# Causal attention of a decoder's first layer: the mask made in the score banks, maxima subtracted by halves

## The chip, the cores and the metric

The kernel runs on one core of one Trainium2 chip. A core has five instruction queues that run side by side: TensorE (PE, with its weight loads shown as PEld), VectorE (DVE), ScalarE (ACT), GpSimd (POOL) and SyncE (SP), the last used here for issuing transfers only. Each queue is worked in order; semaphores tie the queues together. Matrix products land in PSUM, eight banks of 128 x 512 fp32, and everything else lives in SBUF. The metric is the device time of the whole program in microseconds, median of several runs.

## The reference

The program is a decoder of four layers, each with self-attention, cross-attention and a feed-forward part, over x of 8 batches, 128 tokens and 256 features. The change is in the very first part:

```python
q = split_heads(lin(x, Wq, bq))          # x: layer-normed; 16 heads of 16
k = split_heads(lin(x, Wk, bk))
v = split_heads(lin(x, Wv, bv))
attn = jnp.einsum('bhqd,bhkd->bhqk', q, k) * scale          # scale = 1/4
attn = jnp.where(causal[None, None], attn, -jnp.inf)
attn = jax.nn.softmax(attn, axis=-1)
out = jnp.einsum('bhqk,bhkd->bhqd', attn, v)
out = out.transpose(0, 1, 3, 2).reshape(Bx, Tx, Cx)
return lin(out, Wp, bp)
```

Its result is added to x, and the next parts go on from there. Every later part needs the one before, so there is no work that could be done ahead of this one but loads, constants and products of weights.

## The kernel before, in words

**The start.** `decoder` (L2448) issues loads of constants, of x and of the context, and sets a few constants on GpSimd. GpSimd also sends a small table `less_own` to DRAM (L2501) and loads the byte mask of the context, `mu` (L2510), for later layers; VectorE turns it into fp32 (L2513) and derives two more tables (L2514, L2515). `mu` lives in a pool of its own that is closed again, and the weights' pool opens in its place. Then the twelve parts are called one after the other. Outside hand-ordered blocks the framework orders the instructions of each engine by itself; a block under `manual_schedule` keeps the order in which the code gives them.

**The first attention, `l0_attn` (L224).** The weights are loaded by SyncE (`weights`, L96): `w` with four matrices and `r` with biases, followed by the next part's `w` and `r` and two large pieces `st`. After the norm of x and its transposes (L191), eight groups of products (L46, tile `ps_mm`) give the queries `qT` and the keys `kb`; ScalarE and VectorE copy them out of PSUM (L247, L250, L253). `kb` holds every key twice, with the odd or the even head of a pair masked to zero, so that one product over 32 rows gives one head's scores. Then the values `va` are made (L258, L261), with a column of ones beside each head's 16 values: the product with the exponentials gives the sum of a row along with its values.

**The steps.** What follows goes over the 8 batches in a software pipeline: `in_step` (L379) gives, for each step t, each stage for batch t minus the stage's lag, all in one hand-ordered block. The stages, with their lags before the change, are:

- `score` (0): eight products (L209) fill a tile of four PSUM banks, 128 queries by 16 heads by 128 keys; VectorE adds the causal mask from the constants while it copies them to `s` (L280). There is one such tile, so the next batch's scores wait for this copy. In the call for batch 2, `clear_rows` (L1011) is called first: it writes zeros to the 8.4 MB DRAM buffer `rows_in` of a much later part, by a transfer that GpSimd issues (L1014).
- `less_max` (0): VectorE takes each row's maximum (L285), GpSimd subtracts it (L286).
- `exp` (1): ScalarE's exponential over all 16 heads (L301).
- `values` (2): `round_about` (L337) transposes the four groups of heads (L345), ScalarE copies them out (`pT`, L347), and products with `va` (L293) give the tile `ps_po`.
- `copied`, `turn`, `divided`, `project` and the add (3): `ps_po` is copied by ScalarE (L367) and transposed back (L375), VectorE divides by the sums (L312, L316), TensorE projects (L46, tile `ps_o`), VectorE adds to x (L195), and the next norm's statistics are taken (L155, L156) by batch.

With a largest lag of 3, eight batches take eleven steps. PSUM is full: four banks for scores, two for transposes, one for `ps_po`, one for the rest.

Of the kernel before, what the change touches and what calls it, by code (L numbers as in the profile page):

```python
# [8 lines left out]
F32 = mybir.dt.float32  # L9
BF16 = mybir.dt.bfloat16  # L10
# [3 lines left out]
AF = mybir.ActivationFunctionType  # L14
ALU = mybir.AluOpType
AX = mybir.AxisListType

P = 128
# [14 lines left out]
C_ID, C_LE, C_GT, C_CAUS, C_BO16, C_ONES = 0, 128, 256, 384, 512, 640  # L33
# [9 lines left out]
def mm(nc, out, pairs):  # L43

    for i, (lhsT, rhs) in enumerate(pairs):
        nc.tensor.matmul(out, lhsT, rhs, start=(i == 0), stop=(i == len(pairs) - 1))  # L46
# [151 lines left out]
def tok(b):  # L198
    return slice(b * S, (b + 1) * S)


def scores(k, psc, q, kb):


    for r in range(4):
        rows = slice(32 * r, 32 * r + 32)
        rhs = kb[rows]
        n = rhs.shape[1] * rhs.shape[2]
        k.nc.tensor.matmul(psc(r, n), q[rows], rhs, start=True, stop=True)  # L209
# [14 lines left out]
def l0_attn(k):  # L224
    nc, a = k.nc, k.a
    w, r_ = k.weights(a["p0"], a["r0"])
    wq, wk, wv, wp = (w[:, i * 512 : (i + 1) * 512].rearrange("p (c n) -> p c n", c=NC) for i in range(4))
    bq, bk = w[:, 2048:2050], w[:, 2050:2052]
    bv, bp = r_[:, 0:256], r_[:, 256:512]
    _, xnT = k.norm(bp)  # L230
    H, HD = 16, 16
    with k.tc.tile_pool(name="l0a", bufs=2) as wk_:
        qT = wk_.tile([P, NC, T], F32, name="qT", bufs=1)
        kb = wk_.tile([P, NC, 2, T], F32, name="kb", bufs=1)
        va = wk_.tile([P, B, 4, 4, 32], F32, name="va", bufs=1)
        nc.gpsimd.memset(va, 0.0)
        nc.gpsimd.memset(va[:, :, :, :, HD : HD + 1], 1.0)
        bkm = k.sm.tile([P, NC, 2], F32, name="bkm")
        nc.vector.tensor_tensor(
            bkm, bk.unsqueeze(2).to_broadcast([P, NC, 2]), k.m16.unsqueeze(1).to_broadcast([P, NC, 2]), ALU.mult  # L240
        )
        for g in range(2):
            ts_ = slice(g * 512, (g + 1) * 512)
            for o in range(NC):
                pm = k.mmt()
                mm(nc, pm, [(wq[:, c, o * P : (o + 1) * P], xnT[:, c, ts_]) for c in range(NC)])
                nc.scalar.activation(qT[:, o, ts_], pm, AF.Identity, bias=bq[:, o : o + 1])  # L247
                pm = k.mmt()
                mm(nc, pm, [(wk[:, c, o * P : (o + 1) * P], xnT[:, c, ts_]) for c in range(NC)])
                nc.scalar.activation(  # L250
                    kb[:, o, 0, ts_], pm, AF.Identity, bias=bkm[:, o, 0:1], scale=k.m16[:, 0:1]
                )
                nc.vector.tensor_scalar(  # L253
                    kb[:, o, 1, ts_], pm, k.m16[:, 1:2], bkm[:, o, 1:2], ALU.mult, ALU.add
                )
        for b in range(B):
            pv = k.ot()
            mm(nc, pv, [(xnT[:, c, tok(b)], wv[:, c, :]) for c in range(NC)])  # L258
            for o in range(NC):
                cs = slice(o * P, (o + 1) * P)  # L260
                nc.vector.tensor_tensor(  # L261
                    va[:, b, 2 * o : 2 * o + 2, :, 0:HD].rearrange("p j r d -> p r j d"),
                    pv[:, cs].rearrange("p (r j d) -> p r j d", r=4, d=HD),
                    bv[:, cs].rearrange("p (r j d) -> p r j d", r=4, d=HD),
                    ALU.add,
                )
        caus = k.c[:, C_CAUS : C_CAUS + P].unsqueeze(1).to_broadcast([P, H, P])
        k.banks({"tr": 2, "po": 1, "o": 1})
        S_, PO, OS, PB, OB, PY = {}, {}, {}, {}, {}, {}
        act = nc.scalar.copy  # L270

        def score(b):
            if b == 2:
                clear_rows(k)
            psc = k.sct()
            for o in range(NC):
                scores(k, lambda r, n: psc[:, r, o * 256 : o * 256 + n], qT[:, o, tok(b)], kb[:, o, :, tok(b)])
            s = S_[b] = wk_.tile([P, 4, 4, P], F32, name="s", bufs=4)
            sv = s.rearrange("p r g t -> p (r g) t")
            nc.vector.tensor_tensor(sv, psc.rearrange("p r (g t) -> p (r g) t", t=P), caus, ALU.add)  # L280

        def less_max(b):
            sv = S_[b].rearrange("p r g t -> p (r g) t")
            mx = k.sm.tile([P, H], F32, name="mx")
            nc.vector.tensor_reduce(mx, sv, AX.X, ALU.max)  # L285
            nc.gpsimd.tensor_tensor(sv, sv, mx.unsqueeze(2).to_broadcast([P, H, P]), ALU.subtract)  # L286

        def values(b):
            po = PO[b] = k.pot()

            def use(g, pT):
                for r in range(4):
                    nc.tensor.matmul(  # L293
                        po[32 * r : 32 * r + 32, g, :], va[:, b, g, r, :], pT[:, r, :], start=True, stop=True
                    )

            round_about(k, wk_, lambda g: S_[b][:, :, g, :], [act] * 4, use)

        def exp(b):
            sf = S_[b].rearrange("p r g t -> p (r g t)")  # L300
            nc.scalar.activation(sf, sf, AF.Exp, scale=HD**-0.5)  # L301

        def copied(b):
            OS[b] = back(k, wk_, PO[b])

        def turn(b):
            PB[b] = back_turned(k, OS[b])

        def divided(b):
            pb = PB[b].rearrange("p g (r e) -> p g r e", e=32)  # L310
            rec = k.sm.tile([P, 4, 4], F32, name="rec")
            nc.vector.reciprocal(rec, pb[:, :, :, HD])  # L312
            ob = OB[b] = wk_.tile([P, NC, 4, 2, HD], F32, name="ob")
            for o in range(NC):
                js = slice(2 * o, 2 * o + 2)
                nc.vector.tensor_tensor(  # L316
                    ob[:, o].rearrange("p r j d -> p j r d"),
                    pb[:, js, :, 0:HD],
                    rec[:, js, :].unsqueeze(3).to_broadcast([P, 2, 4, HD]),
                    ALU.mult,  # L320
                )

        def project(b):


            ov = OB[b].rearrange("p o r j d -> p (o r j d)").rearrange("p (t s) -> p s t", s=2)
            py = PY[b] = k.ot()
            mm(nc, py, [(ov[:, s_, :], wp[:, s_, :]) for s_ in range(2)])

        in_step(  # L330
            k, B,
            (3, copied), (3, turn), (0, score), (3, divided), (0, less_max),
            (2, values), (1, exp), (3, project), (3, lambda b: k.add_x(b, PY[b])),
        )


def round_about(k, wk_, src, copies, use):  # L337


    done = {}  # L340
    for g in range(6):
        if g < 4:
            pt = k.trt()
            for r in range(4):
                k.nc.tensor.transpose(pt[:, r, :], src(g)[:, r, :], k.ident)  # L345
            done[g] = wk_.tile([P, 4, P], F32, name="pT", bufs=3)
            copies[g](done[g], pt)  # L347
        if g >= 2:
            use(g - 2, done[g - 2])


def all_turned(k, wk_, src, copies):
# [11 lines left out]
def back(k, wk_, po):  # L364

    os_ = wk_.tile([P, 4, P], F32, name="os", bufs=4)
    k.nc.scalar.copy(os_, po)  # L367
    return os_


def back_turned(k, os_):

    pb = k.ot((P, 4, P))
    for g in range(4):
        k.nc.tensor.transpose(pb[:, g, :], os_[:, g, :], k.ident)  # L375
    return pb
# [432 lines left out]
class Heads:  # L809
# [13 lines left out]
    def turn_p(self, u):  # L823

        k = self.k
        pt = self.bank("tr", bufs=2)
        p = self.p.pop(u)
        for j in range(4):
            k.nc.tensor.transpose(pt[:, j, :], p[:, j, :], k.ident)
        self.pT[u] = self.sbuf("pT")  # L830
        k.nc.scalar.copy(self.pT[u], pt)  # L831
# [179 lines left out]
def clear_rows(k):  # L1011

    n = k.rows_in.shape[0] // P
    k.nc.gpsimd.dma_start(  # L1014
        k.rows_in.rearrange("(n p) d -> p n d", p=P), k.zero_rows.unsqueeze(1).to_broadcast([P, n, ROW])
    )
# [451 lines left out]
class L2Keys:  # L1468
# [139 lines left out]
    def values(self, b):  # L1608
        k = self.k
        pv = k.ot((P, 2, D))  # L1610
        for t, wv in enumerate((self.wvm, self.wvd)):
            mm(k.nc, pv[:, t, :], [(k.ctxT[:, b, :], wv)])
        for t in range(2):
            k.nc.scalar.activation(
                self.va[:, b, :, t, 0:16], pv[:, t, :].rearrange("p (h d) -> p h d", d=16), AF.Copy, scale=self.ends[t]
            )
# [1120 lines left out]
```

## Time and profile before

| what | us |
|---|---|
| median of 3 runs | 1948.71 (1945.85, 1948.71, 1960.44) |
| profiled execution, its own time | 1957.12 |
| its span | 1955.3 |
| PE busy in the span | 1717.8 (88%) |
| DVE busy | 1203.0 (62%) |
| ACT busy | 1037.7 (53%) |
| POOL busy | 365.8 (19%) |
| first products of `l0_attn` begin | 25.47 |
| first scores begin | 49.2 |
| last add to x ends | 130.7 |

All durations come from that one profiled execution. In the lines of a timeline the first number is the start from the span's beginning, the second the time that the line took, both in us; then engine, source line, operation, the tiles as out<-in with partitions x elements, and how many instructions the line merges. In square brackets stands how long the engine was idle before it and what ended that. In the lines of the chain of work only start, length and what are given. "SPq" and "POOLq" are the issuing of transfers, and "DMA" is time that passed until a transfer had landed.

### The profile page before, as it was taken

The numbers are of one execution on the slowest core, as the hardware profiler recorded it, in microseconds if no ns is written. First come the engines' busy times: TensorE is split into PE (matmuls) and PEld (weight loads), VectorE is DVE, ScalarE is ACT, GpSimd is POOL, SyncE is SP. The second block draws the span as 40 slices with busy tenths as digits, with TensorE's granted clock in tenths as the row PEclk, the third lists the DMA queues.
The fourth block names the chain that finished last, engine by engine and source line by source line (L and its number), as shares of the span: only waits on it lengthen the run. The fifth ranks groups of instructions, "written<-read, shape, count | busy, mean of one in ns | idle before, by whom it ended". The sixth has DMA issues, their size and how long they took to land.

```text
span 1955.3 us, 25181 instructions
## 1 busy us (share of the span) xinstructions
PE 1717.8 (88%) x9471; PEld 1136.2 (58%) x9477; DVE 1203.0 (62%) x2374; ACT 1037.7 (53%) x1711; POOL 365.8 (19%) x359
## 2 busy tenths in 40 slices
PE   5776977667999986998788989999999997999999
PEld 3453655444666653664466545555555556888667
DVE  4766778856677752326756767677676775454423
ACT  2445854434667741225464377778777763343432
POOL 3543542201121222332002000000000001333200
PEclk9896988878999997998999999999999998999989
DMA  4600026305000022111001110101101004000000
GB/s 135 177 25 1 2 97 209 111 1 215 1 12 6 12 82 105 50 41 51 17 1 36 17 50 18 33 18 34 34 18 34 18 1 162 1 1 1 1 1 22
DMA packets 38970, 90.29 MB, mean 46 GB/s; under 512 B 6865, under 2 KB 19490, under 8 KB 37186
## 3 DMA queue, kind: packets, MB, share of 16 engines
q1 hardware_dynamic: 31266, 69.43, 10.4%
q0 software_dynamic: 5488, 17.67, 3.0%
q8 instruction: 76, 1.25, 0.3%
q10 hardware_dynamic: 2096, 1.57, 0.3%
q14 instruction: 44, 0.36, 0.1%
HBM read 67.15 MB, written 21.51 MB: 45 GB/s over the span
## 4 chain that ended last, share of the span: by engine, by line
PE 68%; DVE 14%; ACT 11%; issue 3%; POOL 2%; DMA 1%; ACTq 0%; DVEq 0%; SPq 0%; POOLq 0%
PE ps_xz L46 9%; PE ps_o L46 7%; PE ps_o L2077 6%; PE ps_o L848 5%; PE ps_mm L46 5%; PE ps_q L46 5%; PE ps_h L46 4%; PE ps_u L46 3%; PE ps_sc L46 3%; PE ps_y L46 2%; PE ps_ty L46 2%; PE ps_xz L1994 2%; DVE mx L511 2%; PE ps_ty L2015 2%; PE ps_sc L209 2%
## 5 line engine op out<-in xcount | busy, mean ns | idle before, releaser
L46 PE MATMUL ps_xz<-xnT,wxz 128*128 128x512 f32 x512 | 237.1, 607 | 0.3 <-ACT ee L1997 0.3
L46 PEld LDWEIGHTS ps_xz<-xnT,wxz 128*128 128x128 f32 x512 | 93.3, 192 | 103.9 <-issue 101.9
L1974 DVE SCALAR_TENSOR_TENSOR xc<-pad,w,xc 128x1024 f32<-128x1024 f32 x96 | 123.1, 1282 | 30.5 <-ACT xc L1968 28.7
L2077 PE MATMUL ps_o<-wo,yg 128*128 128x256 f32 x512 | 128.0, 395 | 1.5 <-DVE yg L2056 1.5
L848 PE MATMUL ps_o<-wvo,uT 128*128 128x256 f32 x512 | 122.6, 383 | 0.0
L848 PEld LDWEIGHTS ps_o<-wvo,uT 128*128 128x128 f32 x512 | 98.5, 193 | 40.7 <-issue 30.3
L1997 ACT ACTIVATE ee<-ps_xz,sgn 128x512 f32<-128x512 f32 x128 | 87.1, 689 | 60.2 <-PE ps_xz L1994 60.2
L2077 PEld LDWEIGHTS ps_o<-wo,yg 128*128 128x128 f32 x512 | 93.5, 192 | 25.4 <-issue 12.9
L2017 DVE TENSOR_TENSOR dtx<-ps_ty,dt 128x512 f32<-128x512 f32 x64 | 41.4, 687 | 90.1 <-PE ps_ty L2015 89.9
L2369 POOL MEMSET gb<- 128x160 f32 x1 | 0.2, 231 | 504.1 <-PE ps_ty L46 504.1
L46 PE MATMUL ps_h<-moe,xT 128*128 x184 | 85.1, 606 | 0.9 <-DVE xT L1244 0.8
L2007 DVE TENSOR_TENSOR ee<-ee,gT 128x2048 f32<-128x2048 f32 x32 | 73.2, 2288 | 8.9 <-ACT ee L2003 8.9
L46 PE MATMUL ps_u<-pT,cx 128*128 128x512 f32 x128 | 70.0, 629 | 6.8 <-ACT pT L831 6.7
L947 ACT ACTIVATE s<-ps_sc,mx,rqs 128x128 f32<-128x128 f32 x128 | 48.1, 456 | 49.5 <-DVE rs_t L129 48.0
L2003 ACT ACTIVATE ee<-ee,sgn 128x1024 f32<-128x1024 f32 x64 | 73.0, 1145 | 0.2
L955 POOL TENSOR_TENSOR s<-s,sums 128x512 f32<-128x512 f32 x32 | 33.3, 1040 | 207.7 <-DVE sums L954 66.6
L512 POOL TENSOR_TENSOR s<-s,mx 128x2048 f32<-128x2048 f32 x16 | 57.8, 3610 | 53.6 <-DVE mx L511 53.6
L1258 DVE TENSOR_TENSOR h<-ps_h,sl 128x512 f32<-128x512 f32 x23 | 15.9, 692 | 82.2 <-PE ps_h L46 82.2
L46 PEld LDWEIGHTS ps_q<-xnT,wqk 128*128 128x128 f32 x512 | 64.3, 199 | 2.8 <-DVE xnT L62 1.0
L46 PE MATMUL ps_q<-xnT,wqk 128*128 128x128 f32 x512 | 64.8, 282 | 0.6 <-DVE xnT L62 0.6
L46 PE MATMUL ps_ty<-ee,dtx 128*64 128x128 f32 x1024 | 63.0, 276 | 2.3 <-DVE ee L2007 2.2
L358 PE MATMUL ps_tr<-consts,s 128*128 128x128 f32 x384 | 55.7, 290 | 8.4 <-ACT s L1726 3.3
(599 smaller groups left out, 4038.3 us busy)
## 6 DMA issues: line engine op xcount, KB each, us to landing
moe<-in_p SPq DMA_DIRECT2D x24, 512.0 KB
rows_in<-zero_rows POOLq DMA_DIRECT2D x1, 8385.0 KB, 34.4
wxz<-in_p9s SPq DMA_DIRECT2D x32, 256.0 KB
fold_vo<-in_p SPq DMA_DIRECT2D x8, 512.0 KB
wvo<-fold_out SPq DMA_DIRECT2D x16, 256.0 KB
wvo<-wvo SPq DMA_DIRECT2D x2, 2048.0 KB
wo<-in_p9s SPq DMA_DIRECT2D x16, 256.0 KB
st<-in_p SPq DMA_DIRECT2D x3, 1024.0 KB
```

What stands on the lines that cost most here:

```text
L46: nc.tensor.matmul(out, lhsT, rhs, start=(i == 0), stop=(i == len(pairs) - 1))
L209: k.nc.tensor.matmul(psc(r, n), q[rows], rhs, start=True, stop=True)
L358: k.nc.tensor.transpose(pt[:, r, :], src(g)[:, r, :], k.ident)
L512: nc.gpsimd.tensor_tensor(sv, sv, mx.unsqueeze(2).to_broadcast([P, 16, P]), ALU.subtract)
L848: k.nc.tensor.matmul(self.po[b], uT[:, j, :], self.wvo[:, 4 * hg + j, :], start=hg + j == 0, stop=hg + j == 6)
L947: nc.scalar.activation(s[:, j, :], psc[:, j, :], AF.Exp, scale=rs[:, j : j + 1], bias=mx[:, j : j + 1])
L1974: nc.vector.scalar_tensor_tensor(XC[n], (PAD[n] if n in PAD else pads[n % 2])[:, :, t : t + S], cw[:, n, t : t + 1], XC[n], ALU.mult, ALU.add)
L1997: nc.scalar.activation(e, pm, AF.Relu, scale=sgn[:, at : at + 1])
L2003: nc.scalar.activation(EE[n][:, h], EE[n][:, h], AF.Exp, scale=sgn[:, at : at + 1])
L2007: nc.vector.tensor_tensor(EE[n], EE[n], gT.unsqueeze(1).to_broadcast([P, 2, B, S]), ALU.mult)
L2017: nc.vector.tensor_tensor(DTX[n][:, bs], pt.rearrange("p (b h d) -> p b h d", b=4, d=HD), dt_[:, bs, 2 * n : 2 * n + 2].unsqueeze(3).to_br ...
L2077: nc.tensor.matmul(PO[b // 2][:, b % 2 * D : (b % 2 + 1) * D], YG[n][:, tok(b)], WO[n // 2][:, n % 2, :], start=False, stop=n == 31 and b ...
```

## The change

Only `l0_attn` is changed, and `round_about` goes, as nothing else used it. The causal mask becomes a bf16 tile; four products of the identity with that tile, repeated four times along the free axis, begin each bank of scores, and the scores are added on top of it in PSUM. VectorE takes the maxima of the heads of half of each bank straight from PSUM and subtracts them on the way to `s`, then does the other half later in the step; GpSimd no longer takes part. The exponential is given by halves too, in the same step as the scores, and everything behind it moves up by one: the largest lag is 2, so that there are ten steps. The order inside a step is a new one, with the transposes and value products of the batch before between the two halves.

```diff
-        caus = k.c[:, C_CAUS : C_CAUS + P].unsqueeze(1).to_broadcast([P, H, P])
+        caus = wk_.tile([P, P], BF16, name="caus", bufs=1)
+        nc.vector.tensor_copy(caus, k.c[:, C_CAUS : C_CAUS + P])
...
         def score(b):
             if b == 2:
                 clear_rows(k)
-            psc = k.sct()
+
+            psc = SC[b] = k.sct()
+            for r in range(4):
+                nc.tensor.matmul(
+                    psc[:, r, :], k.ident_b, caus.unsqueeze(1).to_broadcast([P, 4, P]), start=True, stop=False
+                )
             for o in range(NC):
-                scores(k, lambda r, n: psc[:, r, o * 256 : o * 256 + n], qT[:, o, tok(b)], kb[:, o, :, tok(b)])
-            s = S_[b] = wk_.tile([P, 4, 4, P], F32, name="s", bufs=4)
-            sv = s.rearrange("p r g t -> p (r g) t")
-            nc.vector.tensor_tensor(sv, psc.rearrange("p r (g t) -> p (r g) t", t=P), caus, ALU.add)
-
-        def less_max(b):
-            sv = S_[b].rearrange("p r g t -> p (r g) t")
-            mx = k.sm.tile([P, H], F32, name="mx")
-            nc.vector.tensor_reduce(mx, sv, AX.X, ALU.max)
-            nc.gpsimd.tensor_tensor(sv, sv, mx.unsqueeze(2).to_broadcast([P, H, P]), ALU.subtract)
...
                 for r in range(4):
+                    rows = slice(32 * r, 32 * r + 32)
                     nc.tensor.matmul(
...
+                        psc[:, r, o * 256 : o * 256 + 256],
+                        qT[rows, o, tok(b)],
+                        kb[rows, o, :, tok(b)],
+                        start=False,
+                        stop=(o == 1),
                     )
...
+        def less_max(o):
+            def f(b):
+                js = slice(2 * o, 2 * o + 2)
+                bank = SC[b].rearrange("p r (g t) -> p r g t", t=P)[:, :, js, :]
+                mx = MX[b][:, :, js]
+                nc.vector.tensor_reduce(mx, bank, AX.X, ALU.max)
+                nc.vector.tensor_tensor(
+                    S_[b][:, :, js, :], bank, mx.unsqueeze(3).to_broadcast([P, 4, 2, P]), ALU.subtract
+                )
+
+            return f
+
+        def exp(o):
+            def f(b):
+                sf = S_[b][:, :, 2 * o : 2 * o + 2, :]
+                nc.scalar.activation(sf, sf, AF.Exp, scale=HD**-0.5)
+
+            return f
...
         in_step(
             k, B,
-            (3, copied), (3, turn), (0, score), (3, divided), (0, less_max),
-            (2, values), (1, exp), (3, project), (3, lambda b: k.add_x(b, PY[b])),
+            (0, score), (2, turn), (1, turn_p((0, 1))), (0, less_max(0)), (2, divided), (0, exp(0)),
+            (1, turn_p((2,))), (1, values((0,))), (1, turn_p((3,))), (1, values((1,))), (2, project),
+            (0, less_max(1)), (1, values((2, 3))), (2, lambda b: k.add_x(b, PY[b])), (1, copied), (0, exp(1)),
         )
```

`turn_p` and the new `values` hold what `round_about` did, for the groups that they are given: transposes and a copy by ScalarE, and the products with `va`.

More of the change, by code (lines that the diff above doesn't have):

```diff
@@ L266, in l0_attn @@
                 )
-        caus = k.c[:, C_CAUS : C_CAUS + P].unsqueeze(1).to_broadcast([P, H, P])
+        caus = wk_.tile([P, P], BF16, name="caus", bufs=1)
+        nc.vector.tensor_copy(caus, k.c[:, C_CAUS : C_CAUS + P])
         k.banks({"tr": 2, "po": 1, "o": 1})
-        S_, PO, OS, PB, OB, PY = {}, {}, {}, {}, {}, {}
-        act = nc.scalar.copy
+        S_, MX, SC, PT, PO, OS, PB, OB, PY = {}, {}, {}, {}, {}, {}, {}, {}, {}
         def score(b):
@@ L288, in values @@
-        def values(b):
-            po = PO[b] = k.pot()
-            def use(g, pT):
+            psc = SC[b] = k.sct()
[3 more added lines that the diff above has]
+                )
+            for o in range(NC):
                 for r in range(4):
+                    rows = slice(32 * r, 32 * r + 32)
                     nc.tensor.matmul(
-                        po[32 * r : 32 * r + 32, g, :], va[:, b, g, r, :], pT[:, r, :], start=True, stop=True
-                    )
-            round_about(k, wk_, lambda g: S_[b][:, :, g, :], [act] * 4, use)
@@ L299, in exp @@
-        def exp(b):
-            sf = S_[b].rearrange("p r g t -> p (r g t)")
-            nc.scalar.activation(sf, sf, AF.Exp, scale=HD**-0.5)
+                        psc[:, r, o * 256 : o * 256 + 256],
[3 more added lines that the diff above has]
+                        stop=(o == 1),
+                    )
+            S_[b] = wk_.tile([P, 4, 4, P], F32, name="s", bufs=3)
+            MX[b] = k.sm.tile([P, 4, 4], F32, name="mx")
@@ new lines, in turn_p, with f, values @@
+        def turn_p(some):
+            def f(b):
+                for g in some:
+                    pt = k.trt()
+                    for r in range(4):
+                        nc.tensor.transpose(pt[:, r, :], S_[b][:, r, g, :], k.ident)
+                    PT[b, g] = wk_.tile([P, 4, P], F32, name="pT", bufs=4)
+                    nc.scalar.copy(PT[b, g], pt)
+            return f
+        def values(some):
+            def f(b):
+                if some[0] == 0:
+                    PO[b] = k.pot()
+                for g in some:
+                    pT = PT.pop((b, g))
+                    for r in range(4):
+                        nc.tensor.matmul(
+                            PO[b][32 * r : 32 * r + 32, g, :], va[:, b, g, r, :], pT[:, r, :], start=True, stop=True
+                        )
+            return f
@@ L331, in l0_attn @@
             k, B,
-            (3, copied), (3, turn), (0, score), (3, divided), (0, less_max),
-            (2, values), (1, exp), (3, project), (3, lambda b: k.add_x(b, PY[b])),
-        )
[L337 to L349, printed above, removed]
+            (0, score), (2, turn), (1, turn_p((0, 1))), (0, less_max(0)), (2, divided), (0, exp(0)),
+            (1, turn_p((2,))), (1, values((0,))), (1, turn_p((3,))), (1, values((1,))), (2, project),
+            (0, less_max(1)), (1, values((2, 3))), (2, lambda b: k.add_x(b, PY[b])), (1, copied), (0, exp(1)),
+        )
 def all_turned(k, wk_, src, copies):
```

## The prediction

> **What bounds the kernel now.** The change touches one stage, the first attention of a 1955.3 us span on one core, so I read in this order: the chain of work that ended last, for the first 130 us; the queues of GpSimd and SyncE for the same stretch; the DMA view around the one large GpSimd transfer; VectorE's timeline of one attention step. First the chain (start us, us, what):
>
> ```profile
> 18.95 0.54 issue
> 19.50 0.69 DVE mb L2513
> 20.21 5.22 DMA w<-in_p
> 25.43 0.04 issue
> 25.47 16.07 PE ps_mm L46 x32
> ```
>
> Everything from 20 us on hangs on the weight load `w`, and that load starts as VectorE's cast of the mask (L2513) ends: `w` sits in the memory that the mask tile `mu` leaves, so SyncE waits for the mask's landing and its cast. The queues (start us, us, queue, operation):
>
> ```profile
> 10.54 0.72 POOL L2501 DMA_DIRECT2D less_own<-less_own_rows  x1
> 13.20 0.62 POOL L2510 DMA_DIRECT2D mu<-in_mask_BxS_bf  x1 [1.94 <-DMA less_own<-less_own_rows]
> 27.23 5.50 POOL L184 TENSOR_TENSOR x<-x,r 128x256 f32<-128x256 f32 x8 [13.41 <-DMA r<-in_r]
> ...
> 59.60 3.61 POOL L286 TENSOR_TENSOR s<-s,mx 128x2048 f32<-128x2048 f32 x1 [0.91 <-DVE mx L285]
> 63.15 2.95 POOL L1014 DMA_DIRECT2D rows_in<-zero_rows  x1
> ...
> 20.21 0.33 SPq L101 DMA_DIRECT2D w<-in_p  x1
> ```
>
> The zero fill of `rows_in` (L1014) is issued at 63.15, long after the mask at 13.20, because it stands behind two subtractions of GpSimd. The DMA view, us from issue to landing in the last column:
>
> ```profile
> rows_in<-zero_rows POOLq DMA_DIRECT2D x1, 8385.0 KB, 34.4
> mu<-in_mask_BxS_bf POOLq DMA_DIRECT2D x1, 128.0 KB, 3.2
> q0 software_dynamic: 2176, 8.78, 23.5%
> ```
>
> All GpSimd transfers go through one queue, q0. Last, VectorE in a steady step of the attention:
>
> ```profile
> 87.34 2.29 DVE L280 TENSOR_TENSOR s<-ps_sc,consts 128x2048 f32<-128x2048 f32 x1 [1.48 <-PE ps_sc L209]
> 89.55 0.25 DVE L312 RECIPROCAL rec<-ps_o 128x16 f32<-128x16 f32 x1
> 89.83 0.49 DVE L316 TENSOR_TENSOR ob<-ps_o,rec 128x128 f32<-128x128 f32 x2
> 90.23 2.27 DVE L285 TENSOR_REDUCE mx<-s 128x16 f32<-128x2048 f32 x1
> 92.43 0.41 DVE L195 TENSOR_TENSOR x<-ps_o,x 128x256 f32<-128x256 f32 x1
> 95.00 2.29 DVE L280 TENSOR_TENSOR s<-ps_sc,consts 128x2048 f32<-128x2048 f32 x1 [1.48 <-PE ps_sc L209]
> ```
>
> A step is 95.00 - 87.34 = 7.66 us, with 6.18 us of VectorE work and 1.48 us in which it waits for scores. On the chain, the step runs through ScalarE (exponential, copies of `pT` and `os`) and TensorE. The first scores are made at 49.2, the last `x` is added at 130.7.
>
> **Part 1: the zero fill moves.** `clear_rows` is called inside score(2). Before, GpSimd's hand-ordered subtractions held it back. After, GpSimd has no other work in that block, and the built program has the zero fill directly after the transfer of `less_own` and ahead of the mask's. It waits for nothing: its source is set at 0.87 us. So it is issued at 10.54 + 0.72 = 11.3. In the trace its packets ran from 66.7 to 96.4, that is from 3.5 us after issue and for 29.7 us (8.59 MB, 289 GB/s); at 11.3 that gives 14.8 to 44.5, on engines that are otherwise nearly idle then (mean share 0.14 at 10 to 15 us, 0.07 at 15 to 20).
>
> What does the mask's transfer do behind it? It is now issued at 14.3, once the fill's 2.95 us on GpSimd are over. The row alone says 3.2 us, so 17.5, two us ahead of the cast at 19.5: no cost. But the row is of an empty queue. The Trainium skill, "DMA: Bandwidth & Descriptors", section "Queues, rings and completion order", says that each DMA engine takes the descriptors of one queue in order and shares its time only between queues; its section "SWDGE vs HWDGE vs iDMA" gives GpSimd a single queue, as the page's q0 does. By the rule the mask's 128 KB come after all 8.4 MB. I take the rule, as nothing in this trace shows two GpSimd transfers overtaking each other. The mask then moves at 44.5 and lands some 2 us later (3.2 us less what the issue takes): 46.5. Bounds: 45.3 (right with the last packet and a short tail) to 48.9 (zero fill landed at 11.3 + 34.4 = 45.7, and the full 3.2 after it).
>
> Behind that wait stand, on VectorE, L2513 to L2515, the small product `bkm`, and all copies of `kb`; on SyncE, every weight load of the first layers (`w`, `r`, `w`, `r`, two `st`). Nothing can be done meanwhile: norm and transposes end at 19. Cast 46.55 to 47.2, `w` issued at 47.25, landed after the same 5.22 us at 52.5. TensorE starts at 52.5 instead of 25.47: **+27.0 us** (25.8 to 29.4). What follows shifts as one piece, since the loads that it needs are issued behind `w`. Freeing the engines at 66 to 96 is worth nothing: nothing else moved then. TensorE's longer rest adds no slow start, as it idles 6.6 us ahead of 25.47 today too.
>
> **Part 2: the attention steps.** Removed per batch: L280 and L285 on VectorE (2.29 + 2.27), L286 on GpSimd (3.61), one exponential of 1.91. Added: two maxima and two subtractions of 128x1024 read from the score bank, two exponentials of half size on ScalarE, four 128x512 bf16 matmuls for the mask. L1713 and L1720 do just such a maximum and subtraction from a score bank: 0.415 us for 256 elements and 2.02 us for 1792, so 1.04 ns an element and 1.21 us for 1024, some 1.17 from start to start. Bounds: 1.12 by that line's slope with no more overhead, 1.28 by L1974's mean for 128x1024; over 32 instructions -1.5 to +3.5 us. For the mask the nearest row is the bf16 128x512 group, eight of which took 1.89 us at full clock: 4 x 0.24 = 0.95 us. Bounds: 0.87 (by the slope from five in 1.24 us to those eight) and 1.9 at half clock; over eight steps -0.6 to +7.6 us.
>
> A new loop now sets the step. The four score banks have one buffer, and VectorE reads them until its second subtraction, so the next mask and scores can start only then, and VectorE waits for them: 4 x 1.17 + reciprocal and two products 1.1 = 5.8, then mask 0.95, scores 1.1 (16 records in 1.15 us today), handovers 0.12. That is 7.95 us, against 7.66. The add of `x` with its statistics (1.06 us) lies beside TensorE's 2.1. TensorE has 7.4 us of work in a step (2.05, transposes 16 x 0.14 and 0.6, values 1.5, projection 1.1), ScalarE about 4.8: neither sets it. GpSimd's 28.9 us go, worth nothing by themselves.
>
> From a start at 49.2 as today: first maxima at 51.3, two steps without division at 6.95, five at 7.95, and the norm of the first four batches in between (6 us of VectorE, of which 4.8 show): the eighth batch begins at 109.7, plus 2 us for TensorE's half clock after its first waits (the granted clock is 0.53 at 53 to 63.5 today too, for the same reason): 111.7, against 107.2. From there to the last `x` today's drain takes 23.5 us; with ten steps for eleven I count 5.8 of VectorE, 1 exponential, transposes, copies, values, `os`, turn, division, projection and add, and the previous batch's tail between: 16 to 17.5, so 128.5 to 129. Against 130.7: **-2 us**, with the bounds above -4 to +9. The mask's cast to bf16 (128x128, under 0.3 us) lies in VectorE's idle time near 10 us; uncovered it costs that 0.3. `round_about` going costs nothing.
>
> **The sum.** +27.0 - 2.0 = +25 us. Against the profiled execution (1957.12 us, span 1955.3) this gives 1982; that execution is 8.4 us over the median of the three runs, 1948.71, but inside their 1945.85 to 1960.44. On the median: **1974 us**.
>
> **Rivals.** *The mask overtakes the fill* (not slower by what can be told). If GpSimd's transfers are served side by side, the mask lands near 17.5 and `w` is issued at 20.2 as today; but its queue then shares the engines with 7.0 MB of fill. The loads from 20.2 on are 4.2 MB in some 12.5 us; with half to two thirds of the engines they need 20 to 26, the second `st` lands at 41 to 46 and VectorE, whose sum L599 of `st` stands ahead of three copies of `kb`, holds the last projection's bank: +5 to +10. With -2 that is +6: 1955. It decides if the mask is in before 25 us or so. For it: each transfer has its own semaphore; against it: one queue in the page. *The steps stay at half clock:* TensorE's gaps of 4.9 us after each of the first scores keep it at 0.5 for several steps, the loop then has 4.1 instead of 2.05 and TensorE is itself the bound: +8 for four such steps, 1982. Against it: with 7.4 of 7.95 us busy it has fewer gaps than today, when it recovers at 73.7. *The attention gains what it can:* with VectorE alone as bound (6.9 a step) it ends 9 us earlier, and if the mask overtakes as well, the kernel comes to 1943.
>
> **How the numbers follow.** Forecast 0.80, half clock 0.08, overtaking 0.10, attention at its best with overtaking 0.02. About 1%, 19.5 us, is what a measurement of this kernel can tell from no change. Slower by over 1%: 0.80 x 0.95 + 0.08 = 0.84; within 1%: 0.14; faster: 0.02. The forecast's own range is 1970 to 1982 (+27.0 from 25.8 to 29.4, -2 from -4 to +4, the rest of the upper bound being the half clock's); with half clock at the top and some of the runs' scatter below, 1965 to 1984 leaves about 2 in 10 out.
>
> **What would show it.** The chain has the mask's transfer ahead of L2513, cast at 46 to 48, TensorE's first projection at 52 to 54, GpSimd's zero fill at 11.3. The step is 7.7 to 8.3 us with VectorE waiting about 1 us for scores once a step, and the stretch from first score to last add 77 to 86 us (81.5 today). A cast near 19.5 makes it wrong by 20 us; a stretch over 90 us says that the loop's TensorE part was underrated.

## The result and the profile after

| what | before | after |
|---|---|---|
| median | 1950.83 (4 runs, 1945.85 to 1960.44) | 1976.35 (4 runs, 1973.26 to 1976.99) |
| span of the profiled execution | 1955.3 | 1975.1 |
| first projection of `l0_attn` begins | 25.47 | 52.35 |
| first score product (after: first mask product) | 49.2 | 75.50 |
| last add to x ends | 130.7 | 151.25 |
| from the last add to the end of the span | 1824.6 | 1823.9 |

The changed kernel is slower: the ratio is 1.0122, with a 95% interval of 1.008 to 1.0163. The two spans differ by 19.8 us, and all of that is there when the last x is added: 151.25 - 130.7 = 20.5 us. Behind that point the two executions take the same time within 1 us. The medians differ by more, 25.5 us, because the execution of before that was profiled lies above its median; the interval, worked out on 1950.83 us, runs from 15.6 to 31.8 us and holds both.

The chain of work of the kernel after, in its first 70 us (start us, us, what):

```profile
10.55 0.71 POOL less_own L2521
11.26 2.97 POOL rows_in L1034
14.23 32.03 DMA mu<-in_mask_BxS_bf
...
46.39 0.70 DVE mb L2533
47.11 5.20 DMA w<-in_p
...
52.35 15.60 PE ps_mm L46 x32
```

One link has grown. The mask `mu` takes 32.03 us from issue to landing where it took 3.2, and behind it stand the cast (L2533), the weights `w` and the first projection, as they did before, with unchanged lengths. The queues of GpSimd and SyncE for the first 60 us (start us, us, queue, operation, and in brackets what ended the idle time):

```profile
11.26 2.97 POOL L1034 DMA_DIRECT2D rows_in<-zero_rows  x1
14.23 0.60 POOL L2530 DMA_DIRECT2D mu<-in_mask_BxS_bf  x1
54.07 5.50 POOL L184 TENSOR_TENSOR x<-x,r 128x256 f32<-128x256 f32 x8 [39.24 <-DMA r<-in_r]
...
47.11 0.33 SPq L101 DMA_DIRECT2D w<-in_p  x1
```

The zero fill, which was issued at 63.15 before, is now issued at 11.26, right in front of the mask. SyncE issues `w` at 47.11 instead of 20.21. The DMA view of the stretch from 8 to 70 us (the last figure of the first line is us from issue to landing; that of the second the share of 16 engines):

```profile
mu<-in_mask_BxS_bf POOLq DMA_DIRECT2D x1, 128.0 KB, 32.0
q0 software_dynamic: 2176, 8.78, 49.9%
```

Both transfers are in q0, the only queue of GpSimd's that the page shows: 2176 packets as before, in another order.

Last, VectorE in a steady step of the attention, and at the norm between the batches (the same columns as in the queues):

```profile
101.45 1.22 DVE L299 TENSOR_REDUCE mx<-ps_sc 128x8 f32<-128x1024 f32 x1 [1.21 <-PE ps_sc L284]
102.78 1.23 DVE L300 TENSOR_TENSOR s<-ps_sc,mx 128x1024 f32<-128x1024 f32 x1
103.92 0.25 DVE L346 RECIPROCAL rec<-ps_o 128x16 f32<-128x16 f32 x1
104.20 0.49 DVE L350 TENSOR_TENSOR ob<-ps_o,rec 128x128 f32<-128x128 f32 x2
104.61 1.22 DVE L299 TENSOR_REDUCE mx<-ps_sc 128x8 f32<-128x1024 f32 x1
105.86 1.23 DVE L300 TENSOR_TENSOR s<-ps_sc,mx 128x1024 f32<-128x1024 f32 x1
107.00 0.41 DVE L195 TENSOR_TENSOR x<-ps_o,x 128x256 f32<-128x256 f32 x1
...
109.30 1.23 DVE L299 TENSOR_REDUCE mx<-ps_sc 128x8 f32<-128x1024 f32 x1 [1.21 <-PE ps_sc L284]
...
123.83 0.17 DVE L158 TENSOR_SCALAR ln_var<-ln_mv 128x4 f32<-128x4 f32 x1
```

A step is 109.30 - 101.45 = 7.85 us, with one wait of 1.21 us for scores. TensorE's side of that loop, from its timeline:

```profile
107.14 1.02 PE L278 MATMUL ps_sc<-caus,ident_b 128*128 128x512 bf16 x4 [0.40 <-DVE s L300]
108.09 1.15 PE L284 MATMUL ps_sc<-kb,qT 32*128 32x256 f32 x16
```

TensorE is released by VectorE's last subtraction (L300), makes mask and scores in some 2.1 us, and then VectorE goes on. The whole attention, from the first product in the score banks to the last add, takes 151.25 - 75.50 = 75.75 us, against 130.7 - 49.2 = 81.5 before. Where it gains shows at the eighth batch. Here are its first VectorE operation and the last add to x, first in the kernel before, then, behind the dots, in the changed one, whose first mask product comes last (from TensorE's timeline):

```profile
107.21 2.28 DVE L280 TENSOR_TENSOR s<-ps_sc,consts 128x2048 f32<-128x2048 f32 x1
130.27 0.42 DVE L195 TENSOR_TENSOR x<-ps_o,x 128x256 f32<-128x256 f32 x1 [1.29 <-PE ps_o L46]
...
135.85 1.23 DVE L299 TENSOR_REDUCE mx<-ps_sc 128x8 f32<-128x1024 f32 x1 [2.06 <-PE ps_sc L284]
150.82 0.43 DVE L195 TENSOR_TENSOR x<-ps_o,x 128x256 f32<-128x256 f32 x1 [1.36 <-PE ps_o L46]
...
75.50 1.03 PE L278 MATMUL ps_sc<-caus,ident_b 128*128 128x512 bf16 x4
```

Up to the eighth batch the new attention is the slower one: 135.85 - 75.50 = 60.35 us, against 107.21 - 49.2 = 58.0. The drain behind it takes 15.4 us instead of 23.5. So two things stand in the traces: a start that is 26.3 to 26.9 us later, and an attention that is 5.7 us shorter, all of it in the drain.

### The profile page after: what moved, and what is told of

The parts are those of the page before. It is cut to its first block, busy times and chain, and to the rows that moved or that the text cites. A ratio compares the mean times of both kernels' runs of the same rounds, so it can differ in the third digit from the quotient of the medians.

```text
span 1975.1 us, 25256 instructions
## 1 busy us (share of the span) xinstructions
PE 1715.8 (87%) x9503; PEld 1131.2 (57%) x9509; DVE 1202.7 (61%) x2391; ACT 1038.3 (53%) x1719; POOL 338.2 (17%) x351
## 4 chain that ended last, share of the span: by engine, by line
PE 67%; DVE 14%; ACT 11%; issue 3%; DMA 3%; POOL 2%; SPq 0%; DVEq 0%; ACTq 0%; POOLq 0%
PE ps_xz L46 9%; PE ps_o L46 7%; PE ps_o L2097 6%; PE ps_mm L46 5%; PE ps_o L868 5%; PE ps_q L46 5%; PE ps_h L46 4%; PE ps_u L46 3%; PE ps_sc L46 3%; PE ps_y L46 2%; PE ps_ty L46 2%; PE ps_xz L2014 2%; DVE mx L531 2%; DMA mu<-in_mask_BxS_bf 2%; PE ps_ty L2035 2%
## 5 line engine op out<-in xcount | busy, mean ns | idle before, releaser
L46 PE MATMUL ps_mm<-xnT,w 128*128 128x512 f32 x96 | 47.4, 638 | 35.1 <-DMA w<-in_p 33.3
L1278 DVE TENSOR_TENSOR h<-ps_h,sl 128x512 f32<-128x512 f32 x23 | 15.9, 692 | 82.3 <-PE ps_h L46 82.3
```

## The experiments

The theory: the change consists of two parts that have nothing to do with each other. The late start is the mask's place behind the zero fill in one queue, and it would come with no attention change at all; the new steps alone make the kernel faster. The rival for the first part: the start is late because of something else in the new order, such as the fill's early claim on the DMA engines, or the new cast, so that the place of the mask in the queue is not what decides. The rival for the second part: the 5.7 us come from the fill having left the attention's own time, not from the new steps. Ratios are to the kernel before on the same chip, with 95% intervals.

### The zero fill out of the way, in both kernels

In the changed kernel `clear_rows` moves to the scores of the next attention, where it stands behind two of GpSimd's subtractions:

```diff
         def score(b):          # l0_attn
-            if b == 2:
-                clear_rows(k)
...
         def score(u):          # l0_xattn
+            if u == 2:
+                clear_rows(k)
```

> The changed kernel, but the zero fill is issued in the next attention, behind GpSimd's first two subtractions there. Theory (the mask waits in GpSimd's queue behind the fill): the mask is cast at 19.5 us and TensorE's products start at 25.5 instead of 52.4; the stretch from first score to last add stays at 75.7 us, so the kernel gains 26.9 on the changed one and is 6 us under the kernel before: about 1944, ratio 0.997. Rival (the new steps are what costs, and the start's shift is made up elsewhere): it stays above 1965.

Measured: 1948.67 us (median of 20) against 1955.96 for before, ratio 0.9966 (0.9956 to 0.9976), span 1946.3. Its chain, from 19 us on:

```profile
19.57 0.70 DVE mb L2533
20.28 5.28 DMA w<-in_p
...
25.60 16.55 PE ps_mm L46 x32
```

The start is that of before (19.50, 20.21, 25.47) within 0.15 us, with the new cast and all of the new order in place, so neither of these explains the late start. The last add ends at 125.65, and the attention takes 75.95 us, as in the changed kernel.

The same move was made in the kernel before, to see what the fill's time is worth by itself:

> The kernel before with only the fill moved into the next attention, as in the version with the late fill. Theory: the fill costs nothing in either place, ratio 1.000, last add at 130.7 as before; then the whole gain of the late-fill version is the new attention's. Rival: part of that gain came from taking the fill out from under the first attention; then this kernel is 3 to 6 us faster than before too.

Measured: 1954.12 (20) against 1952.47, ratio 1.0002 (0.9992 to 1.0012); TensorE begins at 25.44, scores at 49.99, the last add ends at 130.24. By the medians, taking the fill out of the old attention changes nothing that can be told. In its trace, though, the old attention takes 130.24 - 49.99 = 80.25 us, and 80.04 in the next run, which has no fill in it either; in the kernel before it took 81.5. So 1.3 to 1.5 of the 5.7 us may have left with the fill, or be scatter of single executions: which of the two stays open. The rival for the second part falls for the rest, 80.25 - 75.95 = 4.3 us, which belongs to the new order of the steps. Between this run and the one before it only the attention differs, and the last add comes 130.24 - 125.65 = 4.6 us earlier in the second; by the ratios the difference is 0.36%, some 7 us, with an uncertainty of about 3.

### The zero fill first, in the kernel before

The reverse: the old attention is kept, and only the fill goes ahead of the mask.

```diff
-            if b == 2:
-                clear_rows(k)
...
-        nc.gpsimd.dma_start(k.less_own, rows)
+        with tc.manual_schedule():
+            nc.gpsimd.dma_start(k.less_own, rows)
+            clear_rows(k)
```

> The kernel before, with only the fill's place changed: issued behind the small table and ahead of the mask, as in the changed kernel. Theory: cast at 46.4 us, everything 26.9 us later, about 1977, ratio 1.014. Rival (the fill's place alone is harmless, its cost comes only with the new attention): under 1960.

Measured: 1977.45 (4) against 1955.96, ratio 1.0116 (1.0097 to 1.0135), span 1978.4. Its chain:

```profile
11.26 2.97 POOL rows_in L1012
14.23 30.38 DMA mu<-in_mask_BxS_bf
...
44.74 0.70 DVE mb L2513
...
45.46 5.18 DMA w<-in_p
...
50.68 16.68 PE ps_mm L46 x32
```

The old kernel with this one transfer moved has the loss: TensorE begins 25.2 us later (26.9 in the changed kernel, whose mask took 1.65 us longer to land), and the last add ends 24.3 us later. The attention of the changed kernel is not needed for it. By the medians alone the two can't be told apart (1.0116 here, 1.0122 for the changed kernel); that the new attention is the shorter one rests on the traces and on the run with the fill late.

### Half of the fill ahead of the mask

If the mask waits for the bytes ahead of it in its queue, half the fill costs about half the wait. The fill was cut: 33 of its 65 blocks stay ahead of the mask, 32 go to the next attention.

```diff
-                clear_rows(k)
+                clear_rows(k, 0, 33)
...
+            if u == 2:
+                clear_rows(k, 33)
```

> The changed kernel with the fill cut in two: 33 of its 65 blocks of rows where the fill stands now, ahead of the mask, the other 32 in the next attention. Theory (the mask waits for the bytes ahead of it in its queue): the wait shrinks with the bytes, packets from 14.8 to 29.9, cast at 31.5 us instead of 46.4, TensorE at 37.4; against the kernel before +12 - 6, ratio 1.003. Rival (a fixed price of such a transfer ahead, not its bytes): cast still above 42.

Measured: 1960.67 (15) against 1952.47, ratio 1.0037 (1.0023 to 1.0051), span 1959.9. The chain:

```profile
11.27 1.90 POOL rows_in L1036
13.16 0.04 issue
13.21 16.98 DMA mu<-in_mask_BxS_bf
...
30.31 0.71 DVE mb L2536
```

The mask lands at 13.21 + 16.98 = 30.2, with the whole fill ahead of it at 46.3, and with none at 16.4 (issued at 13.2, 3.2 us). Half of the bytes cost 14 of the 30 us. The wait goes with the bytes ahead of it.

### The fill early, but the mask not behind it

Two ways of keeping the early fill and freeing the mask. In the first the mask is issued by SyncE:

```diff
-        nc.gpsimd.dma_start(
+        nc.sync.dma_start(
             mu.rearrange("p b s -> p (b s)"), a["mask_BxS2_bf1"].rearrange("b s -> (b s)").partition_broadcast(P)
```

> The changed kernel with the fill where it is, at 11.3 us, but the mask's transfer given to SyncE's queue instead of GpSimd's. Theory (order within one queue): the mask passes the fill and lands by 18; the weights are issued near 20 and share the engines with the fill, so that w lands at 28 to 30 and the second st at 41 to 46: start of the scores 5 to 10 us later than before, attention 6 shorter, 1949 to 1955. Rival (the DMA engines are full, not the queue): the mask lands after 30 here too, and the kernel stays above 1960.

Measured: 1958.74 (12) against 1955.96, ratio 1.0026 (1.0017 to 1.0036), span 1954.5. SyncE's queue and, behind the dots, VectorE's timeline:

```profile
12.99 0.33 SPq L2530 DMA_DIRECT2D mu<-in_mask_BxS_bf  x1
20.42 0.33 SPq L101 DMA_DIRECT2D w<-in_p  x1
...
44.45 2.29 DVE L619 TENSOR_REDUCE part<-st 128x1 f32<-128x2048 f32 x1 [4.97 <-DMA st<-in_p]
48.48 2.29 DVE L619 TENSOR_REDUCE part<-st 128x1 f32<-128x2048 f32 x1 [1.74 <-DMA st<-in_p]
```

The cast is back at 19.71 and `w` is issued at 20.42, with the fill issued at 11.28 as in the changed kernel: it is the queue and not the fill as such that holds the mask. But `w` now lands at 32.4, after 12 us instead of 5.2, and VectorE waits for `st` twice, ahead of the last copies of `kb`. The fill in turn lands 41.8 us after its issue, where 33.1 were taken in the old kernel with the fill first. Two queues share the engines, and what stands on the critical path got less than half of its speed. The first mask product comes at 60.24, 10.5 us later than with the fill late, and the last add at 135.17. The collision was expected, but not its full size: `w` at 28 to 30, the second `st` at 41 to 46 (VectorE waits for it until 48.5) and 1949 to 1955 us, which the measured time exceeds.

In the second the mask is on GpSimd's queue still, but ahead of the fill:

```diff
-            if b == 2:
-                clear_rows(k)
...
+        with tc.manual_schedule():
+            nc.gpsimd.dma_start(
+                mu.rearrange("p b s -> p (b s)"), a["mask_BxS2_bf1"].rearrange("b s -> (b s)").partition_broadcast(P)
+            )
+            clear_rows(k)
```

> The changed kernel with both transfers on GpSimd's queue, the mask ahead of the fill. Theory: the mask lands at 16.5; then as with the mask on SyncE, the weights share the engines with the fill: 1949 to 1955. Rival (any early fill costs the same 27 us, as it takes the engines for 30 us): above 1970.

Measured: 1962.24 (4) against 1955.96, ratio 1.0047 (1.0028 to 1.0066), span 1960.4. The mask lands 3.4 us after its issue at 13.2. The two transfers are the same as in the changed kernel, on the same queue, and only their order differs; the landing moves from 46.3 to 16.6. The loads then collide as in the first way: `w` from 22.48 to 33.90, first mask product at 61.89, last add at 137.5, and again the time lies above the expected 1949 to 1955 us. Some 2 us come from elsewhere: the cast is at 21.77 and not at 19.6. VectorE's timeline (first line) and GpSimd's point to why:

```profile
13.79 3.74 DVE L165 TENSOR_SCALAR xn<-x,ln_mv,ln 128x256 f32<-128x256 f32 x4
...
13.84 2.93 POOL L1032 DMA_DIRECT2D rows_in<-zero_rows  x1
```

With the fill late the same four instructions take 1.38 us; here they take 3.74, while GpSimd is issuing the fill until 16.77. Taken one by one, three of them last about 0.4 us each, and one lasts 2.77 and ends at 16.88. The issue itself was not varied apart from its place.

### GpSimd busy beside VectorE

In the kernel before, the norm between the batches had one odd line, VectorE's L158 on 128x4 numbers. It took 2.75 us, and it takes 0.17 in the changed kernel. VectorE's and, behind the dots, GpSimd's timeline of the kernel before:

```profile
101.22 2.75 DVE L158 TENSOR_SCALAR ln_var<-ln_mv 128x4 f32<-128x4 f32 x1
...
100.34 3.61 POOL L286 TENSOR_TENSOR s<-s,mx 128x2048 f32<-128x2048 f32 x1 [4.05 <-ACT s L301]
```

It ends at 103.97, and GpSimd's subtraction ends at 103.95. To see whether that is chance, the fill-late version was given one GpSimd subtraction of the old size per step, on a tile that nobody reads. The work is added; nothing is left out. The tile is also set to zero once by GpSimd:

```diff
+        idle = wk_.tile([P, H, P], F32, name="idle", bufs=1)
+        nc.gpsimd.memset(idle, 0.0)
...
+                if o:
+                    nc.gpsimd.tensor_tensor(
+                        idle, idle, MX[b].rearrange("p r g -> p (r g)").unsqueeze(2).to_broadcast([P, H, P]), ALU.subtract
+                    )
```

> The late-fill version with one GpSimd subtraction over 128x2048 per step on a scratch tile that nothing reads, started by the step's maxima as the kernel before did it. Theory: VectorE's small operation L158 (0.17 us with GpSimd idle, 2.75 in the kernel before) cannot run while a GpSimd operation does: it takes over 2 us again, the gap of the norm in the steps grows by as much, and the stretch from first score to last add goes from 75.9 to about 78; ratio 0.998 against 0.9966. Rival (L158's 2.75 us came from its place in the old order): it stays under 0.3 us and the stretch at 75.9.

Measured: 1954.34 (12) against 1952.47, ratio 1.0005 (0.9991 to 1.0019), against 0.9966 without the subtraction. VectorE's and GpSimd's timelines:

```profile
99.91 1.48 DVE L158 TENSOR_SCALAR ln_var<-ln_mv 128x4 f32<-128x4 f32 x1
...
97.75 3.61 POOL L304 TENSOR_TENSOR idle<-idle,mx 128x2048 f32<-128x2048 f32 x1 [4.30 <-DVE mx L299]
```

L158 ends at 101.39, GpSimd at 101.36. The dependence is there, though smaller than the over 2 us that were expected, since GpSimd began earlier in the step. The attention grows from 75.95 to 78.5 us. L158 explains 1.3 of these 2.5. Another 1.06 is a longer wait for the scores of the last batch (3.29 instead of 2.23 us). Beside it stands TensorE's clock: TensorE rested 3.16 us behind the norm instead of 1.85, and its next four projections took 2.08 us instead of 1.14, at a granted clock of 0.50 (107 to 111 us). That the longer rest lowered the clock is likely, but was not tried.

This run's first cast is also 2.2 us late (21.77), so its total says less than its stretch. The cause looks like the same thing once more. VectorE's and GpSimd's timelines at the start of this run:

```profile
10.75 2.37 DVE L158 TENSOR_SCALAR ln_var<-ln_mv 128x4 f32<-128x4 f32 x1
...
11.27 1.82 POOL L270 MEMSET idle<- 128x2048 f32 x1
```

L158 ends at 13.12 and GpSimd's setting of the added tile at 13.09; in the changed kernel, without that tile, this L158 takes 0.17 us.

### The mask's products taken out

The causal mask itself is left out here, so that the scores begin their banks; all else is the fill-late version.

```diff
-            for r in range(4):
-                nc.tensor.matmul(
-                    psc[:, r, :], k.ident_b, caus.unsqueeze(1).to_broadcast([P, 4, P]), start=True, stop=False
-                )
...
-                        start=False,
-                        stop=(o == 1),
+                        start=True,
+                        stop=True,
```

> The late-fill version without the four mask products per batch: the causal mask is left out, the scores start their banks themselves. Theory (the step is VectorE's work plus TensorE's mask and scores): the step goes from 7.85 to 6.88 us, VectorE's wait for scores from 1.21 to 0.24, the stretch from 75.9 to about 68.5; ratio 0.993. Rival (TensorE's queue as a whole or ScalarE sets the step): the step shrinks by less than 0.4.

Measured: 1942.34 (6) against 1952.47, ratio 0.9947 (0.9928 to 0.9967). VectorE's timeline of a step:

```profile
77.42 1.23 DVE L293 TENSOR_REDUCE mx<-ps_sc 128x8 f32<-128x1024 f32 x1 [0.26 <-PE ps_sc L278]
...
84.32 1.22 DVE L293 TENSOR_REDUCE mx<-ps_sc 128x8 f32<-128x1024 f32 x1 [0.26 <-PE ps_sc L278]
```

The step falls from 7.85 to 6.90 us, and VectorE's wait from 1.21 to 0.26: by 0.95 each. The attention takes 68.2 instead of 75.95 us. That shows the loop: what TensorE adds between VectorE's last subtraction and its next maximum is paid in full, step by step, at 0.95 us.

## Why the prediction was right, and where a size was off

**Part 1, the fill moved ahead of the mask: right, step by step.** The fill was predicted to be issued at 11.3 (11.26) and the mask at 14.3 (14.23), the mask to land at 46.5 (46.3), the cast to end at 47.2 (47.1), `w` to be issued at 47.25 (47.11) and to land after the same 5.2 us, and TensorE to begin at 52.5 (52.35): +27.0 predicted, +26.9 measured. The step that carried it was the choice between the row (3.2 us, of an empty queue) and the rule of one queue in order, and the rule held: the old kernel with the fill first has the same loss (25.2 us at the start), half the fill has half the wait, and the same two transfers the other way round have none.

**Part 2, the steps: the sign right, the size too small.** -2 us were predicted for the attention, and -5.7 were measured. The shape was right: the eighth batch later and the drain shorter, +4.5 and -6 to -7.5 us predicted, +2.3 and -8.1 measured. (That the drain is shorter for having ten steps instead of eleven is the prediction's reading; no run varied it.) By the prediction's own terms:

| term | predicted | measured |
|---|---|---|
| first product to first maxima | 2.1 | 2.17 |
| two steps without division, with the half clock's 2 us | 15.9 | 16.0 |
| five steps, with the norm between | 44.55 | 42.18 |
| last batch's first maxima to the last add | 16 to 17.5 | 15.4 |

(The last three rows of the measured column are differences of the first maxima, at 77.67, 93.67 and 135.85, and the last add's end.)

The third row is the mis-sized term. The prediction took the norm at 6 us of VectorE, of which 4.8 show, with L158 at the 2.75 us that its row had before. Three steps without a norm took 7.78, 7.85 and 7.86, not 7.95, which is 0.4 us. The two around the norm took 18.69 us where 2 x 7.95 + 4.8 = 20.7 had been set, which is 2.0.

L158's part is 2.75 - 0.17 = 2.58 us, of which some 0.85 were lost again, as VectorE then waited 2.06 us for the eighth batch's scores instead of 1.21. L158 had been long because of GpSimd's subtraction, as the run with the added one shows, and that subtraction is what the change removes. "GpSimd's 28.9 us go, worth nothing by themselves" was the sentence that failed.

The step of 7.95 us was near the measured 7.85 because errors in its sum cancel. The reciprocal and the two products were set at 1.1 us, where the prediction's own lines have 0.68 (89.55 to 90.23) and 0.69 was measured, while the four operations on the score banks took 4.86 us instead of 4 x 1.17, and TensorE's mask and scores with the handovers 2.30 instead of 2.17. The drain's estimate was 0.6 to 2.1 us too long; which of its pieces was over-sized was not tried. And up to 1.5 of the 5.7 us may be the fill's departure or scatter, as the old attention without it showed; the prediction put that at nothing.

**The rivals.** *Overtaking* did not happen. Its price could be measured all the same, by the two versions in which the mask lands early: the first mask product came at 60.24 and 61.89 instead of 49.70, so the sharing costs 10.5 and 12.2 us (2.2 of the latter from the later cast), at or a little over the top of the +5 to +10 that were given. *Half clock for several steps* came true for one batch and part of another: in the changed kernel the second batch's mask products took 1.89 us, at a granted clock of 0.50, those of the next five 1.02 to 1.04, and the eighth's, behind the norm, 1.41, at 0.69. The 2 us that the forecast held for the second batch are what the table shows. *The attention at its best* (6.9 us a step) is what the run without mask products reached, so that size of a step was within reach, but the mask's 0.95 us stand in its way.

**The sum.** In the traces it is +26.9 less 0.6 (the first product began 26.3 later, as the projections took a little less time) less 5.7, which makes the +20.5 of the last add (within the rounding), against +25 predicted. What follows the last add took 1819 to 1825 us in all ten traces, so no part of the sum beyond that scatter lies there. That the median came within 3 us of the forecast is partly luck: 1948.71 + 20.5 is 1969, and the later medians of the kernel before lie higher, between 1950.83 and 1955.96.

**What beats both kernels** is the new attention with the fill where something else holds it back: 0.9966 (0.9956 to 0.9976).

## What to carry to other kernels

When a change takes an engine out of a hand-ordered block, list what stood behind that engine's work in its queue: it is free to move now, and a large transfer may come to stand ahead of a small one on which everything waits. A change of that kind is best measured as two changes, since here a gain of 4 to 6 us in the attention was hidden under a loss of 26 us outside it. When carrying a duration over to the new kernel, ask what ended it: a 128x4 operation of 2.75 us measures its neighbour, not itself.

## What the runs showed of the hardware that was not expected

A small VectorE operation that only reads and writes SBUF can last as long as the GpSimd operation beside it. L158 ended within 0.03 us of GpSimd's subtraction in the kernel before (103.97 and 103.95), in the kernel before with the fill late (104.23 and 104.21) and in the run with the added subtraction (101.39 and 101.36), and took 0.17 us where GpSimd was idle. Beside the added subtraction, the subtraction from PSUM (1.23 us), the add to x (0.41) and the norm's statistics (0.43) ran at their usual length. The Trainium skill, "SBUF — State Buffer", section "Who interferes with whom", says that a VectorE operation in a two-port mode, which a `tensor_scalar` such as L158 can enter, takes a pair of ports that it shares with GpSimd, and that whichever of the two issues first keeps the pair for its whole instruction while the other is blocked. The ends above agree with it; no run here shows which mode L158 ran in, and the start does not always tell who was first: in the run with the added tile L158 is recorded from 10.75 and GpSimd's setting of the tile only from 11.27. The issuing of a large transfer by GpSimd went with the same effect once: 3.74 instead of 1.38 us for four `xn` operations of VectorE, beside an issue of 2.93 us.

A transfer on the critical path that shares the engines with a large one of another queue lost more than half of its speed: `w`, 1.0 MB, took 12 and 11.4 us instead of 5.2.
